# Loads of x for the k|v rows: issued from GpSimd's DMA queue instead of the sync engine's, in a sparse graph-attention layer

## Chip, cores and metric

The kernel runs on one core of one Trainium2 chip. The metric is the device time of one execution in microseconds (us), lower is better. Engines are named as the profile names them: PE is TensorE (PEld its weight loads), DVE is VectorE, ACT is ScalarE, POOL is GpSimd, SP is the sync engine, which issues DMAs and computes nothing. A DMA can be issued from the queue of SP, ACT or POOL.

## What is computed

One layer of graph attention with 4096 sources and 4096 targets, D = 512, eight heads of 64, all in float32. The edge mask `adj` is a 4096 x 4096 int32 matrix with about 0.4% ones. Cut to what matters:

```python
hs = layer_norm(x)                      # sources
ht = layer_norm(h_target)               # targets
q = (ht @ Wq + bq).reshape(T, H, HD) / sqrt(HD)
k = (hs @ Wk + bk).reshape(S, H, HD)
v = (hs @ Wv + bv).reshape(S, H, HD)
logits = where(edge_mask != 0, einsum('thd,shd->hts', q, k), -1e30)
ctx = einsum('hts,shd->thd', softmax(logits), v).reshape(T, D)
ht = layer_norm(ht + ctx @ Wo + bo)
out = layer_norm(x + ht + gelu(ht @ W1) @ W2)
```

## The kernel before, in words

The kernel uses the sparsity: it turns every row of `adj` into a short list of source numbers, sorts the targets by their number of edges, and gathers for each target only the rows of k and v that its list names. It has two parts.

**The front, up to about 270 us**, which the change touches, weaves three streams together:

- *The projection* (`project`). The 4096 rows of x are taken in 16 groups of two tiles of 128 rows (`NG` = 16, `G` = 2). For group n, `request(n)` loads 256 rows (512 KB) into one of five places of a ring buffer in SBUF that the program calls `kv` (`xrows(n)`, places 12 to 16); `measure(n)` takes mean and variance on DVE (L702, L703, L685) and the reciprocal root as a power on POOL (L692); `scale(n)` normalizes on ACT (L917); `turn(n)` transposes on PE (L931) and copies out of PSUM into `h2T` (L937 on DVE for group 0, L941 on ACT for the others); `source(n, j)` multiplies tile j with Wk and Wv (L956, eight matmuls each), copies the product out on ACT (L958) and stores the k|v rows to a DRAM table `kvd` from ACT's queue (L962). In step n the loads of group n+4 are requested, group n+3 is measured, n+1 is transposed and n+2 is scaled.
- *The lists* (`edges`). Each tile of 128 target rows of `adj` comes in four quarters of 512 KB (`quarter`, L720, SP's queue), of which up to eight are held. ACT takes the sign and counts the edges (L740), DVE multiplies by the column number (L747) and takes the largest entries (L749, L768, L770). What is left over is stored from SP's queue (`rest_d`, L780). The lists of the first 16 tiles are sorted (L855 and L872 on PE, L861 on DVE) and scattered to DRAM from POOL (L880).
- *The statistics of h_target* (`moments`): 32 loads of 256 KB on SP's queue (L811), with L702 and L703 on DVE.

The loads of x also go through SP's queue (L901); the very first group is loaded apart, in two halves, ahead of all (L594). The weights Wk and Wv come through ACT's queue at the start (L527).

**The rest, up to the end**, is attention over the sorted targets: POOL gathers k|v rows by list (L994), DVE multiplies and reduces, ACT takes exponentials, PE adds up, and the feed-forward blocks (L1407, L1416) run on PE between them. The first gather needs all of `kvd`.

The order of the instructions on each engine is not written by hand. The program states the steps, `_weave` interleaves the streams by the costs that they yield, and a scheduler then gives each engine one fixed sequence, by its own estimate of when each operand will be there. [...] So moving a DMA to another queue can also change the order on engines that the edit doesn't name.

Of the kernel before, what the change touches and what calls it, by code (L numbers as in the profile page):

```python
# [443 lines left out]
def adj_resnorm_kernel(  # L444
# [33 lines left out]
    nc = tc.nc  # L478
# [51 lines left out]
    def rows(a, g):  # L530
        return a[g * GR:(g + 1) * GR, :].rearrange("(j p) d -> p j d", p=P)

    with tc.tile_pool(name="keep", bufs=1) as keep:
# [17 lines left out]
        with ExitStack() as late:  # L551
# [26 lines left out]
            def xrows(n):  # L578
                return ring[:, 12 + n % 5, :].rearrange("p (j d) -> p j d", j=G)
# [311 lines left out]
            def project(order, t=None):  # L891
# [4 lines left out]
                def request(n, t=None):  # L896
                    if n >= len(order):
                        return
                    if t is None:
                        t = xrows(n)  # L900
                        nc.sync.dma_start(t, rows(x, order[n]))  # L901
                    state[n] = t

                def measure(n):
# [60 lines left out]
                with tc.manual_schedule(engines={mybir.EngineType.DVE}):  # L965
                    request(0, t)
                    measure(0)
                    scale(0)
                    turn(0)
                    request(1)  # L970
                    measure(1)
                    scale(1)
                for n in range(2, 4):
                    request(n)
# [500 lines left out]
            order = list(range(NG))  # L1475
# [108 lines left out]
```

## Time and profile before

| | |
|---|---|
| median of 3 runs | 1751.44 us (1750.71 to 1752.84) |
| profiled execution, its own time | 1753.52 us |
| profiled execution, span | 1751.8 us |
| mean granted clock of TensorE | 0.976 |
| busy: PE, DVE, ACT, POOL | 1657.4 (95%), 1424.3 (81%), 1233.9 (70%), 1022.9 us (58%) |
| moved by DMA | 461.00 MB, mean 263 GB/s |
| L901 on SP's queue | 15 loads of 512 KB, median 8.1 us from issue to landing, first at 1.7 us, last at 193.3 us |

A line of the timeline reads: start in us, duration in us, engine, source line, operation, what it writes <- what it reads, number of instructions merged into the line, and in square brackets how long the engine had been idle just before and what ended that wait. "SPq" and "ACTq" are the queues on which DMAs are issued; their durations are issue times. A line of the waits reads: who waited, for whom, total us, how often, the longest. Durations come from one profiled execution.

### The profile page before, as it was taken

How to read it: one execution, taken by the hardware profiler on the slowest of the kernel's cores; microseconds unless marked ns; L12 is line 12 of the kernel's file. 1: busy time of each engine (PE TensorE's matmuls, PEld its weight loads, DVE VectorE, ACT ScalarE, POOL GpSimd, SP SyncE). 2: the span in 40 equal slices, each digit the busy share in tenths (PEclk: the TensorE clock that was granted, in tenths of full speed). 3: DMA queues.
4: the chain of work that ended last, by engine and by line, in shares of the span. 5: the costliest groups of instructions: out<-in, count | busy, mean ns of one | idle time of the engine just before them, and what ended most of it. 6: DMA issues, size and time to landing. Idle time of an engine off the chain costs nothing. (4 is left out here: it accounts for less than half of the span.)

```text
span 1751.8 us, 22710 instructions
## 1 busy us (share of the span) xinstructions
PE 1657.4 (95%) x6978; PEld 1080.6 (62%) x6978; DVE 1424.3 (81%) x2454; ACT 1233.9 (70%) x3134; POOL 1022.9 (58%) x824
## 2 busy tenths in 40 slices
PE   7999896899999999998789999999999999999997
PEld 3444443677676767666566667666666666666665
DVE  6887796889898989988888998988989788999300
ACT  5776674679678978687567877777878677878311
POOL 1000155657566666878778787777787866774101
PEclk9999998899999999999899999999999999999998
DMA  9999988978888887877888878887877767775000
GB/s 349 382 388 352 362 270 302 337 272 286 295 285 307 299 309 267 289 229 242 269 285 276 291 259 286 296 267 234 269 252 255 254 221 262 225 261 187 25 1 27
DMA packets 141610, 461.00 MB, mean 263 GB/s; under 512 B 18036, under 2 KB 23048, under 8 KB 141480
## 3 DMA queue, kind: packets, MB, share of 16 engines
q0 software_dynamic: 96272, 342.33, 57.8%
q1 hardware_dynamic: 39504, 98.26, 15.8%
q10 hardware_dynamic: 5704, 18.89, 2.7%
q8 instruction: 57, 0.93, 0.2%
q14 instruction: 73, 0.60, 0.1%
HBM read 430.61 MB, written 28.79 MB: 262 GB/s over the span
## 5 line engine op out<-in xcount | busy, mean ns | idle before, releaser
L994 POOL DMA_INDIRECT kv<-kvd,rec x603 | 797.2, 1322 | 303.9 <-issue 114.8
L1407 PE MATMUL pf<-h2T,w 128*128 128x256 f32 (+1 forms) x2304 | 469.8, 358 | 3.5 <-ACT h2T L1192 3.4
L1416 PE MATMUL po<-w,gt 128*128 128x512 f32 x1024 | 465.0, 597 | 3.8 <-ACT gt L1410 3.7
L1407 PEld LDWEIGHTS pf<-h2T,w 128*128 128x128 f32 x2304 | 395.9, 192 | 64.9 <-issue 17.9
L1287 DVE TENSOR_TENSOR kv<-kv,tq 128x1536 f32<-128x1536 f32 (+2 forms) x211 | 351.6, 1677 | 57.3 <-DMA kv<-kvd,rec 49.0
L1268 ACT ACTIVATE kv<-kv,pa 128x64 f32<-128x64 f32 x1520 | 390.6, 337 | 4.0
L1293 DVE TENSOR_REDUCE lg<-kv 128x24 f32<-128x1536 f32 (+2 forms) x211 | 350.4, 1668 | 0.2
L1416 PEld LDWEIGHTS po<-w,gt 128*128 128x128 f32 x1024 | 189.1, 192 | 202.3 <-issue 194.8
L1247 PEld LDWEIGHTS cps<-ident,kv 128*128 128x128 f32 x1828 | 218.1, 144 | 101.9 <-issue 47.1
L1247 PE MATMUL cps<-ident,kv 128*128 128x128 f32 x1828 | 243.0, 279 | 35.0 <-DVE kv L1234 19.4
L1234 DVE TENSOR_TENSOR kv<-kv,p 128x1024 f32<-128x1024 f32 (+1 forms) x211 | 251.2, 1194 | 17.6 <-ACT p L1300 17.5
L692 POOL TENSOR_TENSOR n_rs<-n_ve,mhalf 128x2 f32<-128x2 f32 (+2 forms) x53 | 53.3, 1006 | 336.5 <-DVE n_ve L685 172.7
L740 ACT ACTIVATE kv<-kv 128x1024 uint8<-128x1024 int32 x128 | 134.3, 1052 | 55.8 <-DMA kv<-in_adj_dram 17.6
L1410 ACT ACT_TABLE_LOAD x108 | 138.6, 1283 | 1.9
L1410 ACT ACTIVATE gt<-pf 128x512 f32<-128x512 f32 x128 | 76.4, 597 | 79.0 <-PE pf L1407 75.6
L956 PE MATMUL pq<-wk,h2T 128*128 128x512 f32 x256 | 120.9, 617 | 2.1 <-DMA wk<-in_L_gnn_Wk_dram 1.1
L1157 PE MATMUL t<-wo,rb 128*128 128x512 f32 x256 | 119.1, 609 | 3.9 <-DVE rb L1144 3.9
L956 PE MATMUL pq<-wv,h2T 128*128 128x512 f32 x256 | 115.6, 594 | 5.9 <-ACT kv L958 3.0
L1047 PE MATMUL t<-wq,tq 128*128 128x512 f32 x256 | 116.7, 600 | 3.5 <-ACT tq L1040 3.5
L749 DVE MAX8 cand<-kv 128x8 uint16<-128x171 uint16 (+1 forms) x384 | 108.3, 324 | 1.0
L1300 ACT ACTIVATE p<-lg 128x24 f32<-128x24 f32 (+2 forms) x179 | 39.0, 218 | 88.5 <-DVE lg L1293 84.7
L956 PEld LDWEIGHTS pq<-wv,h2T 128*128 128x128 f32 x256 | 48.2, 190 | 68.8 <-issue 56.4
(165 smaller groups left out, 1584.1 us busy)
## 6 DMA issues: line engine op xcount, KB each, us to landing
kv<-in_adj_dram SPq DMA_DIRECT2D x128, 512.0 KB, 7.0
kvd<-tq ACTq DMA_DIRECT2D x23, 512.0 KB, 7.1
kv<-kvd,rec POOLq DMA_INDIRECT x603, 5.8
kv<-in_L_gnn_h_target_dram SPq DMA_DIRECT2D x32, 256.0 KB, 6.6
w<-in_L_gnn_W_dram SPq DMA_DIRECT2D x8, 1024.0 KB, 9.6
kv<-in_x_dram SPq DMA_DIRECT2D x15, 512.0 KB, 8.1
kvd<-kv ACTq DMA_DIRECT2D x9, 512.0 KB, 6.7
rest_d<-gid SPq DMA_DIRECT2D x32, 96.0 KB, 5.0
```

Source lines behind the costliest of these rows:

```text
L740: nc.scalar.activation(sg, a, AF.Sign, accum_out=dpart[:, i, h:h + 1])
L956: nc.tensor.matmul(pkv, hT[:, kc, j * P:(j + 1) * P], w[:, kc, :], start=kc == 0, stop=kc == KC - 1)
L994: issues[:] = [nc.gpsimd.indirect_dma_start(out=dst, out_offset=None, in_=table[:, :], in_offset=bass.IndirectOffsetOnAxis(ap=idx, axis=0) ...
L1157: nc.tensor.matmul(pa, ct[:, c, :], wo[:, c, :], start=False, stop=c == KC - 1, skip_group_check=True)
L1234: nc.vector.tensor_tensor(v4, v4, p[:, j0:j0 + m, :].unsqueeze(3) .to_broadcast([P, m, H, HD]), ALU.mult)
L1247: nc.tensor.matmul(cps[:, c, :], kv[:, j, D + c * P:D + (c + 1) * P], ident, is_transpose=True, start=j0 + j == 0 and c == 0, stop=j0 + n ...
L1268: newest[:] = [nc.scalar.mul(v, v, pa[:, hd:hd + 1]).ins]
L1287: nc.vector.tensor_tensor(kv[:, :n, :D], kv[:, :n, :D], tq[:, :D].unsqueeze(1) .to_broadcast([P, n, D]), ALU.mult)
L1293: logits[:] = [nc.vector.tensor_reduce(lg[:, :n, :], kv[:, :n, :D].rearrange("p j (h d) -> p j h d", h=H), AX.X, ALU.add).ins]
L1407: nc.tensor.matmul(pf[:, k, :], w1[(f0 + k) // KC][:, kc, (f0 + k) % KC * P:((f0 + k) % KC + 1) * P], h2T[:, kc, :w], start=kc == 0, stop= ...
L1410: nc.scalar.activation(gt, pf, AF.Gelu_apprx_tanh)
L1416: nc.tensor.matmul(po[j], gt[:, k, j * P:(j + 1) * P], w2[(f0 + k) // KC][:, (f0 + k) % KC, :], start=False, stop=f0 + k == FC - 1, skip_g ...
```

## The change

The 15 loads of L901 are issued from GpSimd's queue instead of SP's. The two halves of the first group (L594) stay on SP's queue, as do the loads of `adj` and `h_target`. Sizes, places and the number of loads are the same. (In the attention part other rows of x are gathered by GpSimd, as before.)

```diff
                 def request(n, t=None):
                     if n >= len(order):
                         return
                     if t is None:
                         t = xrows(n)
-                        nc.sync.dma_start(t, rows(x, order[n]))
+                        nc.gpsimd.dma_start(t, rows(x, order[n]))
                     state[n] = t
```

## The prediction

> **What bounds the kernel now.** I read the 40 slices first, then stretches of 20 us, then the waits and the timeline of the stretches in which TensorE is not full. The chain that ended last is of no use here: on this page it holds only the final few instructions.
>
> ```profile
> span 1751.8 us, 22710 instructions
> ...
> PE   7999896899999999998789999999999999999997
> ...
> DMA  9999988978888887877888878887877767775000
> ```
>
> TensorE is full in nearly every slice. What it loses at the front is never regained, because behind the front it has no idle time to give back. So the change is worth what it does to the end of the k|v projection (first matmul at 10.97 us, last ones at about 269 us).
>
> ```profile
> core 0: us, PE busy (x) PEld busy (x) DVE busy (x) ACT busy (x) POOL busy (x), PEclk, DMA share, GB/s
> 0.00:20.00 20.00, 11.52 (x25) 5.33 (x25) 5.82 (x20) 3.98 (x6) 4.07 (x19) 1.00 0.92 333
> 20.00:40.00 20.00, 16.06 (x40) 7.35 (x40) 19.32 (x77) 15.95 (x28) 2.78 (x4) 0.91 0.98 371
> 40.00:60.00 20.00, 20.00 (x60) 9.73 (x59) 18.25 (x75) 16.89 (x34) 0.74 (x2) 1.00 1.01 382
> ...
> 200.00:220.00 20.00, 15.98 (x42) 7.14 (x41) 10.78 (x38) 12.16 (x23) 0.69 (x1) 0.92 0.96 344
> ```
>
> Columns: stretch, busy us by engine, granted clock, share of the DMA engines, GB/s. Two things hold at once: TensorE is nearly full, and so are the DMA engines (shares of 0.92 to 1.04 up to 240 us). GpSimd is nearly idle. Now the idle stretches of TensorE:
>
> ```profile
> 10.97 5.84 PE L956 MATMUL pq<-wk,h2T 128*128 128x512 f32 x8 [1.08 <-DMA wk<-in_L_gnn_Wk_dram]
> ...
> 23.81 0.33 PE L931 MATMUL t<-ident,kv 128*128 128x128 f32 x1 [3.57 <-ACT kv L917]
> ...
> 25.33 5.29 PE L956 MATMUL pq<-wk,h2T 128*128 128x512 f32 x8
> ...
> 208.77 3.70 PE L956 MATMUL pq<-wv,h2T 128*128 128x512 f32 x8 [1.74 <-ACT kv L958]
> ...
> 215.95 0.32 PE L872 MATMUL cps<-oh,lower 128*128 128x384 bf16 x1 [1.63 <-DVE kv L861]
> 216.12 5.29 PE L956 MATMUL pq<-wk,h2T 128*128 128x512 f32 x8
> ```
>
> ```profile
> 19.86 0.43 DVE L747 TENSOR_TENSOR kv<-kv,lio 128x512 uint16<-128x512 uint16 x1 [8.07 <-ACT kv L740]
> ...
> 174.21 1.29 DVE L702 BATCH_NORM_STATS2 n_st<-kv 128x6 f32<-128x512 f32 x2 [7.00 <-DMA kv<-in_x_dram]
> ...
> 204.63 1.29 DVE L702 BATCH_NORM_STATS2 n_st<-kv 128x6 f32<-128x512 f32 x2 [4.74 <-DMA kv<-in_x_dram]
> ```
>
> The first hole (20.2 to 23.8 us) comes from the adjacency: VectorE stands 8.07 us on the sign of the first adjacency quarter, which landed at 18.68 us behind four x loads. The later ones do come from x: VectorE waits 7.00 and 4.74 us for rows whose loads went out late (164.29 and 193.26 us, behind stalls of SP's queue) and took 9.9 and 11.3 us to land.
>
> [...] The shares near 1.0 agree that there is no spare bandwidth. [...] The trace: eight matmuls take 3.43 us, but 5.13 us after the hole at 20 us.
>
> **The change, part by part.** Fifteen 512 KB loads leave SP and join GpSimd. I also compared the order of instructions in the two built programs: TensorE's is the same; VectorE's, ScalarE's, GpSimd's and SP's differ in the projection stage only, and everything behind it stands alike.
>
> *Issue.* SP loses 15 x 0.42 us. GpSimd gains 15 x about 1.0 us (the nearest rows: 0.95 us for an indirect DMA of 128 rows, 0.55 us for a direct one of record rows), 8 to 25 us in all, under its 187 us of idle time in the first 260 us. Its rsqrt powers (L692) now stand behind x loads. A load of x waits for TensorE's transposes of the group five before, long done, so the powers do not wait: 0, bounds 0 to +2.
>
> *The start, the largest term.* With x1 to x4 off SP, the four adjacency quarters and h_target follow x0 directly. The scheduler reckoned with that: ScalarE's first work is now the sign of adjacency quarter 0, and VectorE's has statistics of three h_target tiles, three small copies and that quarter's L747 **ahead of the four L937 copies that make h2T for the first matmul**. They run at 9.29 us before; now they wait for the third h_target tile. When does it land? Ahead of it on SP: x0 0.52, four quarters 2.10, three tiles 0.79 MB; on ACT wk and wv, 2.10; together 5.51 MB. GpSimd's x1 to x5 take part with 0.5 to 2.6 MB; [...] I take 2.0, so 7.5 MB. The DMA view in slices of 1.5 us adds up to 7.06 MB at 21 us and 7.64 at 22.5, so 7.5 is moved at 22.1. The lag is known: the first h_target tile had 7.08 MB ahead (21.1 us) and landed at 23.2, so 2.1 us. The third tile lands at about 24.2 (20.5 with 0.5 MB of x, 25.8 with all). Then L702 0.69, copies and L747 1.8, the first L937 0.54: first matmul at about **27.3 us** instead of 10.97, later by 16.3 (12.6 to 18).
>
> *What that gives back at once.* Before, 14.4 us lie between the first matmuls of the first two source tiles, and the second's first group is 1.7 us slow: 16.1. After, scale(1) is ready in time: one cold group 5.7, one warm 3.4, transposes 0.9: 10.0. That returns 6.1; net **+10.2** (+6.5 to +12).
>
> *The late x waits go.* With x loads issued four groups ahead on a queue that no adjacency load blocks, the 7.00 and 4.74 us waits vanish. TensorE had lost to them 1.49 (at 175.7) and 1.74 (at 207.0), and behind the second, since VectorE's scan ran late, 0.66 and 1.63 plus a slow group of 1.7: **-7.2** (0 to -7.2). Other holes (1.32, 1.03, 0.75, 0.56) belong to engine order: taken as staying, bound -3.7.
>
> *What is late next.* In ScalarE's new order up to five more signs stand ahead of the middle source tiles (63 instead of 58 at the nineteenth): 2.6 MB more adjacency, 7 us at 380 GB/s, must land before those tiles are copied out. TensorE's ten us of delay cover that; if a good part of the start were not lost, this would bite. I take +1 (0 to +4). kvd stores, gathers and attention keep their order and move with the end of the stage.
>
> Sum: +10.2 - 7.2 + 1 = +4, bounds about -4 to +17. The profiled execution took 1753.5 us against a median of 1751.4, 2.1 above it; its span is 1751.8. I put the shift on the median. Because the late gain is the less sure of the two large terms (another wait may take part of those holes), I lean to +5: 1756.5.
>
> **Rivals.** *The forecast (0.58):* the start costs more than the late holes return: +3.5 to +13, at +5 about 1756.5. *Even (0.24):* the third h_target tile lands at about 22 us [...]: +8 - 7.2, 1752. For it: the price of GpSimd's share is the least known figure. Against: the 3.4 MB on SP are needed whatever GpSimd does. *Faster (0.18), the other side:* x early enough ends not only the x holes but the small ones too (-10.9), while h_target lands at 20.5 us (+6.5): -4.5, about 1747. It decides for faster once the first matmul starts before about 20 us, or before 24 us with all late holes gone. For it: 19.0 us of VectorE's waits are x's, and VectorE is over 90% busy in the stretches from 20 to 60 us. Against: only 3.2 us of those waits reached TensorE directly. [...]
>
> **How the numbers follow.** 0.2% is 3.5 us, about what a measurement of this kernel can tell from no change. Slower 0.58, same 0.24, faster 0.18. The range 1748 to 1765 leaves a tenth on each side; the likeliest case alone would have 1755 to 1765.
>
> **What would show it.** Right: first L956 matmul at 24 to 29 us and eight or more us of VectorE idle on h_target just before; the second source tile within 11 us of it; no x wait over 2 us after 60 us; the last L956 at 271 to 278 us and the same distance from there to the end. Wrong: first matmul before 20 us; or new waits of ScalarE on adjacency in the middle (150 to 190 us), which would push it above 1765; or the last L956 before 267 us.

## The result, and the profile after

The changed kernel takes **1780.62 us** (median of 6 runs, 1776.10 to 1783.94) beside 1751.70 us for the kernel before on the same chip: ratio 1.0148, 95% interval 1.0122 to 1.0173, so 26 us slower (21 to 30; the two medians lie 29 us apart). The prediction said slower, 1756.5 us, range 1748 to 1765. The direction was right and the size was not.

The page of the kernel after, span and slices (tenths of each of 40 slices that TensorE and the DMA engines were busy):

```profile
span 1778.9 us, 22736 instructions
...
PE   4988899699899999998899999999999999999996
...
DMA  9999867978988897877888888877887767675000
```

Before, TensorE's row began 7999896899: the first slice (44 us) has lost three tenths, the third and fourth one each. The stretches (busy us by engine, granted clock, share of the DMA engines, GB/s):

```profile
core 0: us, PE busy (x) PEld busy (x) DVE busy (x) ACT busy (x) POOL busy (x), PEclk, DMA share, GB/s
0.00:20.00 20.00, 2.49 (x9) 1.61 (x9) 2.35 (x11) 6.14 (x9) 7.90 (x24) 1.00 0.87 321
20.00:40.00 20.00, 11.53 (x29) 5.58 (x30) 14.29 (x49) 5.49 (x11) 2.83 (x4) 1.00 0.94 327
100.00:120.00 20.00, 15.48 (x42) 7.05 (x41) 13.05 (x50) 9.83 (x20) 0.00 (x0) 0.94 0.87 330
200.00:220.00 20.00, 16.39 (x45) 7.55 (x44) 10.28 (x47) 9.35 (x17) 5.00 (x3) 1.00 0.69 265
```

In the first 20 us TensorE and VectorE do almost nothing, while the DMA engines are nearly as full as before (0.87, 0.92). From 100 us on TensorE has holes (idle stretches) that the kernel before did not have; at 200 us even the DMA engines have room. The queue's own waits say why: SP's next load of adj waits for a place that the sign has to free. The first line is of the kernel after, the second of the kernel before:

```profile
SPq L720 <- ACT kv L740: 64.0, 32, 18.3
...
SPq L720 <- ACT kv L740: 22.9, 19, 5.1
```

The holes, in TensorE's timeline:

```profile
28.47 5.61 PE L956 MATMUL pq<-wk,h2T 128*128 128x512 f32 x8 [13.71 <-DVE h2T L937]
...
119.58 6.13 PE L956 MATMUL pq<-wv,h2T 128*128 128x512 f32 x8 [4.52 <-ACT tq L958]
...
191.72 5.40 PE L956 MATMUL pq<-wk,h2T 128*128 128x512 f32 x8 [3.02 <-ACT tq L958]
...
218.77 5.40 PE L956 MATMUL pq<-wk,h2T 128*128 128x512 f32 x8 [3.61 <-ACT h2T L941]
...
291.77 3.60 PE L956 MATMUL pq<-wv,h2T 128*128 128x512 f32 x8
```

The last line began at 266.04 us before: 25.7 us of the 27.1 us by which the span grew are lost by here, and what follows only moves with it (first gather of k|v rows 277.82 before, 303.24 after).

VectorE's timeline at the start of the kernel after:

```profile
7.34 0.18 DVE L639 COPY cols<-t 128x20 f32<-128x20 f32 x1 [0.80 <-PE t L638]
23.19 0.69 DVE L702 BATCH_NORM_STATS2 n_st<-kv 128x6 f32<-128x512 f32 x1 [15.67 <-DMA kv<-in_L_gnn_h_target_dram]
...
26.40 0.70 DVE L702 BATCH_NORM_STATS2 n_st<-kv 128x6 f32<-128x512 f32 x1 [0.53 <-DMA kv<-in_L_gnn_h_target_dram]
...
27.88 0.99 DVE L937 TENSOR_SCALAR h2T<-t,cols 128x256 f32<-128x256 f32 x2
```

This is the start as predicted: the copies of h2T(0) stand behind three statistics of h_target. TensorE's transposes for them were done at 14.76 us; VectorE, idle from 7.52 to 23.19 us for the first of the three, took up the copies at 27.88. And VectorE's waits over the front (0 to 300 us: total, times, longest):

```profile
DVE n_st L702 <- DMA kv<-in_L_gnn_h_target_dram: 32.4, 10, 15.7
DVE kv L747 <- ACT kv L740: 19.9, 2, 16.8
DVE n_st L702 <- DMA kv<-in_x_dram: 16.8, 4, 9.3
DVE gid L761 <- DMA rest_d<-gid: 7.5, 4, 2.2
```

The same two waits in the kernel before:

```profile
DVE n_st L702 <- DMA kv<-in_x_dram: 19.0, 5, 7.0
...
DVE n_st L702 <- DMA kv<-in_L_gnn_h_target_dram: 1.9, 3, 0.8
```

So x, the thing that was given a queue of its own, is waited for about as long as before, and h_target, which stayed on SP, is waited for seventeen times as long. 15.3 of its 32.4 us lie after the start. One late hole, step by step (VectorE, then ScalarE):

```profile
105.82 0.69 DVE L702 BATCH_NORM_STATS2 n_st<-kv 128x6 f32<-128x512 f32 x1 [5.25 <-DMA kv<-in_L_gnn_h_target_dram]
...
110.63 0.69 DVE L702 BATCH_NORM_STATS2 n_st<-kv 128x6 f32<-128x512 f32 x1 [1.50 <-DMA kv<-in_L_gnn_h_target_dram]
...
117.21 1.06 ACT L740 ACTIVATE kv<-kv 128x1024 uint8<-128x1024 int32 x1 [6.42 <-DVE cand L749]
```

VectorE waits for two tiles of h_target, which SP issued at 93.61 and 100.47 us and which landed 12.2 and 10.1 us later. What the new order did here can be counted in the timelines: ahead of the first of these two statistics VectorE has 26 products L747, where it had 32 in the kernel before, while SP has 32 loads of adj ahead of that tile's load in both kernels. The statistic moved ahead and its load did not. The maxima L749 that free a place for the next sign come after these waits in VectorE's order and end at 117.1 us; ScalarE has idled 6.42 us for them; the copy L958 of a finished product stands behind that sign, and TensorE, which needs its PSUM, goes on at 119.58.

For the experiments a small table is of use: when the first matmul of a source tile starts, read from TensorE's timeline (not profile lines; us).

| source tile | before | after | e13 old order, x on POOL | e14 new order, x on SP | e17 old start, new rest | e18 new start, old rest |
|---|---|---|---|---|---|---|
| 0 | 10.97 | 28.47 | 21.08 | 26.27 | 21.44 | 28.25 |
| 1 | 25.33 | 38.22 | 32.07 | 36.89 | 32.42 | 37.98 |
| 6 | 63.12 | 74.31 | 68.16 | 72.97 | 68.51 | 74.07 |
| 14 | 125.42 | 148.39 | 130.46 | 154.21 | 147.25 | 136.37 |
| 22 | 188.50 | 218.77 | 189.57 | 224.33 | 213.51 | 195.33 |
| 31 | 262.60 | 288.34 | 261.90 | 291.30 | 280.61 | 267.02 |

From before to after the shift is 11.2 us at tile 6 and 25.7 us at tile 31.

### The profile page after: what moved, and what is told of

Read it like the earlier page. It is cut to its first block, busy times and chain, and to the rows that moved or that the text cites. A ratio compares the mean times of both kernels' runs of the same rounds, so it can differ in the third digit from the quotient of the medians.

```text
span 1778.9 us, 22736 instructions
## 1 busy us (share of the span) xinstructions
PE 1661.5 (93%) x6978; PEld 1083.6 (61%) x6978; DVE 1422.1 (80%) x2454; ACT 1233.6 (69%) x3134; POOL 1027.9 (58%) x839
## 3 DMA queue, kind: packets, MB, share of 16 engines
q1 hardware_dynamic: 35424, 90.39, 14.6%
## 5 line engine op out<-in xcount | busy, mean ns | idle before, releaser
L994 POOL DMA_INDIRECT kv<-kvd,rec x603 | 786.8, 1305 | 303.8 <-issue 116.5
L740 ACT ACTIVATE kv<-kv 128x1024 uint8<-128x1024 int32 x128 | 134.3, 1052 | 63.5 <-issue 30.0
L956 PE MATMUL pq<-wk,h2T 128*128 128x512 f32 x256 | 122.9, 625 | 25.1 <-DVE h2T L937 13.7
L1157 PE MATMUL t<-wo,rb 128*128 128x512 f32 x256 | 117.1, 601 | 4.8 <-DVE rb L1144 4.8
L749 DVE MAX8 cand<-kv 128x8 uint16<-128x171 uint16 (+1 forms) x384 | 107.7, 325 | 0.9
L956 PEld LDWEIGHTS pq<-wk,h2T 128*128 128x128 f32 x256 | 49.8, 200 | 84.0 <-issue 49.9
```

Source lines behind the costliest of these rows:

```text
L740: nc.scalar.activation(sg, a, AF.Sign, accum_out=dpart[:, i, h:h + 1])
L956: nc.tensor.matmul(pkv, hT[:, kc, j * P:(j + 1) * P], w[:, kc, :], start=kc == 0, stop=kc == KC - 1)
L994: issues[:] = [nc.gpsimd.indirect_dma_start(out=dst, out_offset=None, in_=table[:, :], in_offset=bass.IndirectOffsetOnAxis(ap=idx, axis=0) ...
```

## Experiments

All ratios are to the kernel before on the same chip, with a 95% interval. The runs stand on several chips, on which the kernel before had medians of 1750.42 to 1753.52 us, so kernels from different chips are compared by their ratios, not by their times. (Ratio and medians of one comparison can differ by up to 3 us.)

### Which loads: the first four, or the other eleven

```diff
-                        nc.gpsimd.dma_start(t, rows(x, order[n]))
+                        (nc.gpsimd if n < 5 else nc.sync).dma_start(t, rows(x, order[n]))   # e1
+                        (nc.sync if n < 5 else nc.gpsimd).dma_start(t, rows(x, order[n]))   # e2
```

> Only the first four of the 15 loads (x groups 1 to 4) go through GpSimd's queue, the other eleven through SP's. Theory (two separate losses, both made by the order in which work stands: +11 at the start, where the copies of h2T(0) stand behind three h_target statistics on VectorE, and +14.5 in holes after 100 us, where VectorE waits for late loads of h_target and of x group 15): the start loss stays, first L956 at 26 to 29 us; the late loss goes, since the late loads of x are back on SP between those of adj and h_target. 1763 us (1758 to 1768). Rival 1 (a load on GpSimd's queue costs by itself, in proportion to the loads moved): 4/15 of 29, 1759, with holes spread over the four loads. Rival 2 (the late holes follow from the late start, which throws the streams out of step): about 1780, as the full change.

> The other half: groups 1 to 4 on SP's queue, groups 5 to 15 on GpSimd's. Theory: the start is as in the kernel before (first L956 near 11 us, second source tile near 27), the late holes stay with long waits of VectorE for h_target and for x group 15: 1766 us (1760 to 1772). Rival 1 (cost per load): 11/15 of 29, 1773. Rival 2 (all from the late start): 1752.

e1: 1765.36 us, 1.0073 (1.0046 to 1.0101). e2: 1760.82 us, 1.0046 (1.0026 to 1.0066). e1 has the late first matmul (27.10 us), e2 does not (11.13), and has holes of 2.8 to 3.0 us at 89, 127 and 182 us instead. Neither half is harmless, so the late start is not the whole cause (rival 2). Cost per load would ask for less from four loads than from eleven, and e1 lost no less. But each variant also gets an order of its own, so these two cannot tell the queue from the order.

### The start's order mended

```diff
-                    with behind(newest if i >= NA else []):
+                    with behind(newest if i >= NA else acts[3:4] if n < 4 else []):
-                    with behind(logits):
+                    with behind(logits or (nms[1:2] if n < 4 else [])):
-                stats(ip, t, mvh[:, i, :], "n0")
+                with behind(nms[1:2] if i < 2 else []): stats(ip, t, mvh[:, i, :], "n0")
```

(`acts` and `nms` collect the instructions of L917 and L697; the first statement is the sign L740, the second the product L747, the third the h_target statistics.) e3 is this on the full change, e4 on the kernel before.

> The full change, with the start's order mended: the signs (L740) of the first four quarters of adj stand behind the normalization of x group 1 on ScalarE, their products (L747) and the first two h_target statistics behind n_nm of group 1 on VectorE, so nothing of adj or h_target stands ahead of h2T(0) or of group 1. Theory: the start loss of 11 goes, and with it up to 7 more that the kernel before itself loses at 20 to 24 us; the late loss stays: 1767 us (1761 to 1772), first L956 below 13 us. Rival 1 (the queue costs by itself): above 1772. Rival 2 (the late holes follow from the late start): 1745 to 1752.

> The same mended start with all loads of x on SP's queue. Theory: the 5.6 us hole of the kernel before at 20 to 24 us and the slow group after it go, the rest is as before: 1746 us (1743 to 1752). The difference from the full change with the mended start is then the late loss alone, 14 to 20 us. Rival 1 says the same of this kernel, and also that difference. Rival 2 expects no difference between the two.

e3: 1768.87 us, 1.0103 (1.0074 to 1.0132). e4: 1754.13 us, 1.0013 (1.0001 to 1.0026), 8 us above what was expected. e4's second source tile did start at 21.19 us instead of 25.33, and the gain was gone by tile 14 (130.79 against 125.42): the scheduler had planned the later part anew too. In e3 the first matmul did not come below 13 us but at 20.66, and TensorE's wait names a second cause: Wk had not landed.

```profile
20.66 5.87 PE L956 MATMUL pq<-wk,h2T 128*128 128x512 f32 x8 [10.92 <-DMA wk<-in_L_gnn_Wk_dram]
27.81 3.70 PE L956 MATMUL pq<-wv,h2T 128*128 128x512 f32 x8 [1.29 <-DMA wv<-in_L_gnn_Wv_dram]
```

The kernel after has it as well, hidden under the longer wait for h2T. The DMA issues of its first 40 us say that Wv took 22.9 us from issue to landing:

```profile
wv<-in_L_gnn_Wv_dram ACTq DMA_DIRECT2D x1, 1024.0 KB, 22.9
```

It was 12.0 us before. With x on GpSimd, SP's queue begins with adj at 1.71 us instead of 6.10, and three queues are at work where two were: by 16.2 us, when Wv had landed before, ACT's queue, which carries the weights, has moved 1.01 MB instead of 2.11, SP's and GpSimd's together 3.93 MB where SP's alone had moved 2.99. The prediction had reckoned what x on GpSimd does to h_target on SP's queue, and not what it does to the weights on ACT's.

### The weights ahead of adj, and three changes of the later part

e11 is e3 with Wk and Wv on SP's queue, ahead of adj:

```diff
-            wk = load_w(kvw, Wk, "wk", nc.scalar)
-            wv = load_w(kvw, Wv, "wv", nc.scalar)
+            wk = load_w(kvw, Wk, "wk", nc.sync)
+            wv = load_w(kvw, Wv, "wv", nc.sync)
```

> The full change with the mended start, and the loads of Wk and Wv moved from ScalarE's queue to SP's, ahead of the first load of adj. In the full change with the mended start, VectorE was ready but the first L956 still came only at 20.66 us, having waited 10.92 us for Wk. Theory: with x on a queue of its own, SP begins with adj and h_target at once, and these share the transfer rate with the weights, which land 10 us later than before. If so, the weights ahead of adj land earlier: first L956 at 11 to 15 us, second source tile at 22 to 26, and about 6 us less in all: 1763 us (1757 to 1768). Rival (the weights are late because GpSimd's x loads take the rate, whatever stands in SP's queue, or the rate as such is short): first L956 still at 17 to 21 us, 1769.

First matmul at 11.79 us, second source tile at 23.21; 1761.61 us, 1.0063 (1.0043 to 1.0083). With the weights ahead of adj in the line the first matmul is 8.9 us earlier than in e3, so it was mostly their place that made them late. 11 us of loss remain with a start better than that of the kernel before.

```diff
+                        (nc.sync if n == 15 else nc.gpsimd).dma_start(t, rows(x, order[n]))   # e5
-                while asked and len(asked) > NT - 4 - i:
+                while asked and len(asked) > NT - 7 - i:                                      # e6
-                nc.sync.dma_start(hrow(i), h_target[i * P:(i + 1) * P, :])
+                nc.gpsimd.dma_start(hrow(i), h_target[i * P:(i + 1) * P, :])                  # e10
```

> The full change, with only the last load of x (group 15) left on SP's queue. In the full change GpSimd issued it at 203.5 us, behind the 128x32 power of the h_target statistics, which itself waits for the last h_target tile; VectorE then waited 9.31 us for it, and TensorE had a hole of 3.61 us at 218.8 us and a slow group after it. Theory: this wait goes, the hole goes, 1776 us (1772 to 1779). Rival: the load is one of several that are late at that place; the wait moves to the next one and the time stays at 1780.

> The full change, with the loads of h_target asked for seven tiles ahead instead of four (of eight places). Theory (the holes after 100 us come from h_target loads that stand behind adj loads on SP, which wait for places): VectorE's waits for h_target after 60 us fall from about 17 us to under 5, the holes at 119.6, 148.4 and 191.7 us shrink, about 8 us are won: 1773 us (1766 to 1778); the start stays at 28 us or gets 1 to 2 us worse. Rival 1 (the queue of GpSimd itself costs) and a rival that the waits for h_target only cover waits for adj or x: waits for adj or x grow by what those for h_target lose, 1780.

> The full change, and also the 32 loads of h_target on GpSimd's queue, so that none stands behind a load of adj. Theory: VectorE's waits for h_target after 60 us fall under 4 us; at the start no h_target statistic stands ahead of h2T(0) any more, but the product of the first quarter of adj does and the weights still come late, so the first L956 comes at 20 to 24 us. About 6 us less at the start and 8 later: 1766 us (1758 to 1773). Rival 1 (each load on GpSimd's queue costs): slower than the full change, above 1785.

e5: 1774.80 us, 1.0123 (1.0094 to 1.0153), some 4 us better than the full change by the two ratios, whose intervals overlap; in the trace the hole at 218.8 us is gone, tiles 20 to 22 take 14.6 us instead of 18.4. Its cause is seen in the full change on GpSimd, where the last load stands behind a power of 32 columns, and this behind a smaller one for which GpSimd had stood idle, waiting for VectorE's statistics:

```profile
196.66 0.71 POOL L692 TENSOR_TENSOR n_rs<-n_ve,mhalf 128x2 f32<-128x2 f32 x1 [18.39 <-DVE n_ve L685]
198.07 5.51 POOL L692 TENSOR_TENSOR n_rs<-n_ve,mhalf 128x32 f32<-128x32 f32 x1 [0.70 <-DVE n_ve L685]
203.54 0.75 POOL L901 DMA_DIRECT2D kv<-in_x_dram  x1
```

VectorE then waits 9.31 us for that load, until 211.40.

e6: 1765.75 us, 1.0080 (1.0051 to 1.0109), better than expected, and not where expected: the holes between 113 and 149 us stay (tile 14 at 149.03), VectorE still waits 10.8 us for h_target between 80 and 130 us, and the gain comes after tile 18 (tile 22 at 210.20 instead of 218.77).

e10: 1773.62 us, 1.0120 (1.0090 to 1.0151), against 1766 expected. VectorE's waits over the front:

```profile
DVE kv L747 <- ACT kv L740: 29.3, 5, 16.9
DVE gid L761 <- DMA rest_d<-gid: 17.0, 6, 5.1
DVE n_st L702 <- DMA kv<-in_x_dram: 15.9, 7, 4.9
...
DVE n_st L702 <- DMA kv<-in_L_gnn_h_target_dram: 2.6, 1, 2.6
```

Waits for h_target are all but gone, as said, and others have taken their place: signs, `rest_d`, x. (The weights were late too: Wv was waited for until 31.42 us.) Taking away the load that is waited for did not take away the loss.

### Order and queue told apart

So far each kernel changed the queue and the order together. Here the order is held. `wanted` lists, for VectorE, ScalarE, SP and GpSimd, the instructions of the front in the order in which they stand in one of the two kernels; x loads are in no list. TensorE has no list; in e13 its order came out as in the kernel before.

```diff
+    for e, seq in wanted.items():
+        mine = [i for i in nc.cur_bb.bb.instructions if str(i.engine) == "EngineType." + e
...
+        for a, b in zip(seq, seq[1:]):
+            tc.add_manual_dep(mine[b], mine[a].name, mybir.DependencyInfo(
+                mybir.DependencyClass.NoSync, mybir.DependencyReason.DATA), reason="order")
```

The edges are meant to fix the order and to wait for nothing. e13 has x on GpSimd and the order of before; e14 x on SP and the order of after; e15 is e13 with the weights on SP's queue ahead of adj, as in e11.

> The full change (all 15 loads of x on GpSimd's queue), but the order of the other instructions of the front on VectorE, ScalarE, SP and GpSimd is that of the kernel before, written down as a chain of edges; only where the x loads stand is left to the scheduler. Order and queue are so told apart. Theory (the loss is the new order, but for the weights: SP starts with adj at once, so Wk and Wv share the transfer rate and come some 9 us later): first L956 at 18 to 22 us, second source tile 5 to 7 us later than in the kernel before, no loss after that: 1758 us (1752 to 1764). Rival 1 (the queue itself): 1772 or more, with waits for x longer than in the kernel before. Rival 3 (order is all, the weights don't matter): 1752.

> The counterpart: all loads of x on SP's queue, the front's other instructions on VectorE, ScalarE, SP and GpSimd in the order of the full change. Theory: the copies of h2T(0) stand behind three h_target statistics and the first product of adj again, first L956 at 24 to 29 us; the holes after 100 us come back too: 1774 us (1766 to 1782). Rival 1 (the queue itself): 1752 to 1756, since the queue is the old one.

> All loads of x on GpSimd's queue, the old order on the other engines, and Wk and Wv loaded from SP's queue ahead of adj. Theory: both causes are gone, first L956 at 11 to 14 us, second source tile at 24 to 28: 1752 us (1746 to 1757). Rival 1: 1772 or more. If the late loads of x on a free queue are worth the 7 us that the prediction gave them, it is 1746.

| | order of before | order of after |
|---|---|---|
| x on SP | 1751.70 us (before; 1750.42 on the chip of e13 and e14) | e14: 1782.68 us, 1.0173 (1.0147 to 1.0198) |
| x on GpSimd | e13: 1749.97 us, 0.9995 (0.9979 to 1.0011) | 1780.62 us, 1.0148 (1.0122 to 1.0173) |

**The loss is the order's.** In the old order x on GpSimd's queue costs nothing that can be measured, and rival 1 (the queue) is out; in the new order x on SP loses as much as x on GpSimd. It loses it by other waits, though. VectorE's in e14:

```profile
DVE n_st L702 <- DMA kv<-in_x_dram: 32.6, 6, 8.8
DVE n_st L702 <- DMA kv<-in_L_gnn_h_target_dram: 25.8, 4, 16.0
```

Most of it after the start is for x here (30.1 us, h_target 9.9), so e14 shows that this order is bad for either queue, not that one wait makes both losses. The kernel before with its own order written down as edges was not run; that the edges themselves cost or save nothing is likely, since e13 and e14 each agree with the kernel of the same order without them, but it is not shown.

e13 had been expected at 1758 us and came below its range: the expectation let the late weights cost the total 6 us, rival 3 nothing. (e14 came just above its range, 1766 to 1782.) Late the weights are, as in e3 (TensorE's timeline):

```profile
21.08 5.07 PE L956 MATMUL pq<-wk,h2T 128*128 128x512 f32 x8 [9.93 <-DMA wk<-in_L_gnn_Wk_dram]
```

By the table above e13 is 5.0 us behind at tiles 6 and 14 and 0.7 us ahead at tile 31: what it loses to the weights comes back. It comes from x (VectorE's waits over the front):

```profile
DVE gid L761 <- DMA rest_d<-gid: 9.7, 4, 4.4
...
DVE n_st L702 <- DMA kv<-in_L_gnn_h_target_dram: 5.3, 4, 3.2
DVE n_st L702 <- DMA kv<-in_x_dram: 4.4, 3, 2.5
```

The 19.0 us of waits for x have become 4.4 (the last load of x goes out at 172.2 us, ahead of the 128x32 power; before at 193.3, in the full change at 203.5); some of it went into `rest_d` (3.7 before) and h_target (1.9 before). e15 ended at 1749.27 us, 0.9994 (0.9978 to 1.0011); its first matmul came at 15.01 us and its tile 31 at 259.48, 3.1 us earlier than before. The weights are still late in it (TensorE waits 4.33 us for Wk), with the place in line that gave 11.79 us in e11; the second and third load of x on GpSimd went out at 2.31 and 3.07 us here and at 6.38 and 7.18 there, so x on GpSimd seems to have a part in the weights' lateness.

### Which part of the order

The lists of one kernel up to about 60 us (the 15th L747, the 16th L740, the 22nd L720), those of the other behind; x on GpSimd in both.

```diff
     wanted = {
-        "DVE": [      # e13: all from the order of before
+        "DVE": [      # e17: the first 150 from before, the others as in after; ScalarE 60, SP 37
+        "DVE": [      # e18: the first 159 from after, the others as in before; ScalarE 54, SP 41
...
```

> All loads of x on GpSimd's queue; VectorE, ScalarE and SP follow the order of the kernel before up to the 15th product (L747), the 16th sign (L740) and the 22nd load of adj (L720), about 60 us, and the order of the full change from there. Theory (start and later part of the order cost each on their own): the start is that of the full change with the old order (second source tile near 32 us), the later part takes as long as in the full change, 214 us from source tile 6 to tile 31 instead of 194: last L956 20 us later than in the kernel before, 1770 us (1762 to 1778). Rival (the later holes follow from the start): 1750 to 1755.

> The other way round: the order of the full change up to the same places, the order of the kernel before from there; x on GpSimd's queue. Theory: first L956 at 27 to 29 us, tile 6 near 74 us as in the full change, and 194 to 200 us from there to tile 31: 1760 us (1754 to 1766). Rival (the later holes follow from the start): 1778 or more.

e17: 1769.32 us, 1.0089 (1.0058 to 1.0120). e18: 1758.36 us, 1.0037 (1.0022 to 1.0052). Both came as the theory said. By the ratios, beside e13's 0.9995, the late part of the order costs about 16 us and its start 7; together 24, where the full change stands 27 above e13: the two add up to within 3 us, less than the intervals are wide. In the traces: from tile 6 to tile 31 the full change takes 214.0 us and e17 212.1, but e18 193.0 and e13 193.7 (before: 199.5). The later holes do not follow from the late start. VectorE's waits in e17:

```profile
DVE n_st L702 <- DMA kv<-in_L_gnn_h_target_dram: 25.7, 8, 5.6
DVE kv L747 <- ACT kv L740: 24.3, 4, 20.8
...
DVE n_st L702 <- DMA kv<-in_x_dram: 4.6, 3, 2.4
```

and in e18, where the one long wait for h_target is that of the start (13.7 us of TensorE's time at 28.25):

```profile
DVE n_st L702 <- DMA kv<-in_L_gnn_h_target_dram: 16.0, 3, 14.4
...
DVE n_st L702 <- DMA kv<-in_x_dram: 2.5, 1, 2.5
```

So with x on GpSimd the new order of the later part brings waits for h_target (5.3 us in e13) and longer ones for signs (13.5 in e13). The timelines show what changed places: in e17 and in the full change 29 statistics of h_target stand ahead of the 45th product L747 on VectorE, in e13, e18 and the kernel before 22. In e17 and e14 TensorE's own transposes stand a little differently from before, so a small part of their loss may be that. Which of the moved instructions of the later part does it was not tried; e10 warns against a short answer, and so does e14.

### A faster version?

e16 is the kernel before, in its own order, with the first three signs and the first L747 and L749 moved behind group 1. e19 is the old order with groups 1 to 4 of x on SP and 5 to 15 on GpSimd. e20 is both.

```diff
+                        (nc.gpsimd if n > 4 else nc.sync).dma_start(t, rows(x, order[n]))   # e19, e20
```

> All loads of x on SP's queue and the order of the kernel before, with one thing moved: the first three signs (L740) stand behind the normalization of x group 1 on ScalarE, and the first product (L747) and maximum (L749) of adj behind n_nm of group 1 on VectorE. In the kernel before, TensorE has a hole of 3.57 us at 23.8 us for them, and the second source tile starts at 25.3 us. Theory: it starts at 21 us, the front runs 4 to 6 us earlier from there and keeps it: 1747 us (1743 to 1751). Rival: what is won at the start is lost again where VectorE waits for loads of x (7.0 and 4.7 us after 160 us), since the transfers are no earlier: 1752, as the kernel before with the mended start, where the scheduler had planned the rest anew.

> The order of the kernel before, with groups 1 to 4 of x on SP's queue in their old places and groups 5 to 15 on GpSimd's. Theory (the late x loads on a queue of their own are worth the 5 to 7 us of the prediction, if the order stays and the weights are not held up): second source tile at 25 us, VectorE's waits for x under 6 us instead of 19.0, tile 31 near 257 us instead of 262.6: 1746 us (1741 to 1750). Rival: what x no longer waits for, adj and rest_d wait for: 1751.

> As the last one, and the first three signs and the first product and maximum of adj behind group 1, as in the run that moved them alone (there the start was 4 to 6 us earlier and all was given back where VectorE waited for x). Theory: with earlier x loads it is not given back: second source tile at 21 us, tile 31 near 252 us: 1742 us (1736 to 1748). Rival: the front is held by the transfers, and the gain is given back to waits for adj: 1747 to 1751.

| | median, ratio | tile 1 | tile 31 | first gather of k\|v rows |
|---|---|---|---|---|
| before | | 25.33 | 262.60 | 277.82 |
| e16 | 1753.05, 1.0019 (1.0006 to 1.0033) | 21.29 | 263.89 | 279.04 |
| e19 | 1752.53, 1.0010 (0.9995 to 1.0025) | 26.28 | 258.99 | 273.69 |
| e20 | 1753.28, 1.0003 (0.9983 to 1.0022) | 22.08 | 258.83 | 272.60 |

e16 gave all back, as its rival said: VectorE waits 20.1 us for x. e19 shows the predicted gain in the front (x waited for 2.5 us, tile 31 earlier by 3.6) and none in the total; e20 brings the front 5.2 us forward, and the total does not follow either. The forecasts of a gain, e4's among them, were wrong, and no version here is shown to beat the kernel before. Later ends of the front were passed on about in full (e18 +4.4 us at the first gather and +6.5 by the ratio; e17 +17.1 and +16; after +25.4 and +26). The earlier ends of e19 and e20 were not: the first gather came 4.1 and 5.2 us sooner, and the intervals leave a gain of at most 0.9 and 3.0 us. (e15's 3.7 us at the first gather could still be hidden in its interval.) What holds the rest back then stays open: behind the first gather the rest takes 1465 us (e11) to 1481 us (e19) in the single traces of all these kernels, a spread wider than the few us in question.

## Why the prediction was wrong, step by step

- *The start: right in size, incomplete in cause.* Predicted: first matmul at 27.3 us and +10.2 net. Measured: 28.47 us and +11.2 at tile 6. VectorE waited 15.67 us for h_target, and the second source tile came 9.75 us after the first. Left out were the weights: with nothing of adj or h_target ahead of h2T(0), the first matmul still started only at 20.66 and 21.08 us (e3, e13). The 2.0 MB put down for GpSimd's queue were the author's estimate; in the trace it moved 2.58 MB up to 22.5 us, and ACT's queue with the weights 1.65 instead of 2.11. Of the 11 us at tile 6, 5.0 are there in the old order too, with late weights (e13); the other 6 come with the new order of the start (e18).
- *"The late x waits go", -7.2: the gain exists, somewhat smaller, but its condition was not met.* With the old order it is there: from tile 6 to 31 e13 and e18 take 5.7 and 6.5 us less than the kernel before, and e19, whose start is not late, 4.3. In the full change x is still waited for 16.8 us, the longest wait being 9.31 us. The load of group 15 had been taken to be free of any block on GpSimd; it stands behind a 5.51 us power there, and behind GpSimd's wait for the statistics before it. The prediction had looked at what x loads do to the powers behind them, not at what a power does to a load.
- *"What is late next", +1 (0 to +4): this is the step that failed.* It counted the signs that move ahead on ScalarE, and put nothing for VectorE, where statistics of h_target move ahead of products and maxima of adj. At the hole before 119.58 us the load of such a statistic had not moved ahead with it: VectorE waits for it, and the maxima that free the places of the signs come late. The new order of the later part costs about 16 us (e17 against e13, by the ratios), or 21 us in the traces (214.0 us from tile 6 to 31, against 193.0 in e18 with the same start). The text did name a sign by which it would be wrong: new waits of ScalarE on adjacency between 150 and 190 us and a time above 1765. ScalarE does idle 6.33 us before a sign at 190.05 us, but the profile names no load of adj for it; VectorE's maxima L749 had ended just before, at 189.97, after a wait of 5.77 us for h_target.
- *Issue on GpSimd, 0: right.* Its issues took 0.72 to 0.91 us each, under idle time; the median from issue to landing is 8.5 us against 8.1 on SP.
- *"Behind the front it has no idle time to give back": right for losses.* For gains up to 5 us no run showed it.
- *The sum.* In the traces the 25.7 us at tile 31 split into +11.2 at the start, +21.1 for the later part of the order and -6.5 for x. *The rivals:* the even case wanted the third h_target tile at 22 us; it was used at 26.40. The faster case decided from a first matmul before 20 us, or before 24 us with all late holes gone; it came at 28.47, and the late weights alone put it past 20.

## What to carry to other kernels

Where a scheduler fixes the order, an edit to one DMA is an edit to every engine's order: compare the orders first, and price every instruction that now stands behind one that waits, not only those that the edit names. To learn what the edit itself is worth, hold the old order and change only the queue; here that turned 26 us into nothing. And where one stream gets a queue of its own, name the load that then comes late: here it was the weights, for which TensorE waited until 20.66 and 21.08 us (e3, e13) instead of 10.97.

## Not expected of the hardware

A load of 512 KB of x occupied GpSimd for 0.72 to 0.91 us at issue, and SP's queue for 0.42 us (median); yet from issue to landing the two hardly differ (median 8.5 and 8.1 us), with the DMA engines' share at 0.87 to 1.04 in the stretches up to 200 us. With a third queue at work TensorE waited for two 1 MB loads until 20.66 and 27.81 us (e3), which had landed at 10.97 and 16.2 before; what came sooner was adj, wanted later: ScalarE waited for its first quarter until 10.60 us in the full change, and until 18.68 before.
